# The last sums of an adaLN, fast-weight and expert block on one Trainium2 core: by halves of blocks, with the residual added on GpSimd

## The chip, the cores and the metric

The kernel runs on one core of a Trainium2 chip. The metric is the time of one launch on the device in microseconds. The engines are named as the profile names them: PE (TensorE), DVE (VectorE), ACT (ScalarE), POOL (GpSimd), SP (SyncE, which here only issues transfers). ACT and POOL issue transfers as well, each in a queue of its own, between their other instructions.

## The reference

The input x has 4 sequences of 1024 tokens of 128 features, 4096 tokens in all, in float32. Two sublayers follow each other, each with a layer norm whose shift and scale come from a small condition vector, and each with a gate (ga, gb) on what it adds to x:

```python
h = _layernorm(x) * (1 + ca) + sa
x = x + ga * _L0_attn_ref(h, ...)   # a two-layer network trained token by token, then asked
h = _layernorm(x) * (1 + cb) + sb
x = x + gb * _L0_ffn_ref(h, ...)    # 8 experts, the best 2 of each token, and a shared expert
```

The second sublayer is the one at issue. For each token the router's two largest probabilities are the gates of two experts; the sublayer's output is SCALE * (shared expert + gate0 * expert0 + gate1 * expert1).

## The kernel before, in words

The kernel has four stages: a front part with the first layer norm and the key and value projections; a scan that does the token-by-token training in windows (67 to 562 us of the profile, L498 to L700); the second layer norm and the router; and the experts. The order of every engine's instructions is the order of the program text.

**The scan** matters here only for what it shows of operations that run side by side. In each window DVE does, among others, `mT` from the two SBUF tensors `ae` and `th` (L621), `u` from a PSUM and an SBUF tensor (L530) and `ae` from a PSUM and an SBUF tensor (L650). POOL copies `dl` and `el` (L692, L693) and, in `add_changes`, does `ch` as a difference of two tensors (L547), `sq` and `va` as squares of one tensor (L548, L551) and three sums into `sums` (L555).

**The expert stage.** Tokens are sorted by expert into 71 tiles of 128 rows. For each tile, rows are gathered from `h_tab` (POOL, an indirect transfer, L1081), sent through the expert's two layers (L1108, L1112, L1120), and the result `yg` is scattered (POOL, L1125) into the DRAM table `y_tab`, at row 2 * token + k, k being 0 or 1 for the token's first or second expert. So a token's two rows lie beside each other, 1 KB together. The shared expert is added into `x_sb` in SBUF along the way (L945, L946), so that `x_sb` already holds all but the two experts' parts. The tensors `hs_all`, the shared expert's activations, are dead when the last tile is done.

**The last sums** are L1179 to L1203, and the change is there. The 4096 tokens are 8 blocks of 512, a block being 4 groups of 128 tokens over the partitions.

- Fetch (L1182): block j's rows of `y_tab` are fetched into the dead `hs_all[j]`, 512 KB in a transfer. Even blocks go by SP's queue, odd ones by ACT's. All eight are issued ahead of everything else. The first waits for the last scatter into `y_tab`.
- ACT multiplies the second expert's row by its gate in place (L1195), 128x128 in an operation, four for a block.
- DVE multiplies the first expert's row by its gate and adds (L1196, four for a block, into a tile `o`), multiplies the block by `gb` (L1199, 128x512), and adds `x_sb` (L1202, 128x512).
- Store (L1203): SP sends the 256 KB of `o` to the output. There are three buffers for `o`, so the fourth block waits until the first store has landed.

Every transfer tells its end on a semaphore; the program uses eight of them in turn for the transfers of SP and ACT, and a transfer that takes one up again waits until the earlier transfer on it has landed. After the eight fetches the eight stores take them up again.

Of the kernel before, what the change touches and what calls it, by code (L numbers as in the profile page):

```python
# [10 lines left out]
F32 = mybir.dt.float32  # L11
AF = mybir.ActivationFunctionType
ALU = mybir.AluOpType
# [4 lines left out]
P = 128  # L18
LR = 0.001
EPS = 1e-5  # L20
TOP_K = 2
# [4 lines left out]
def kernel(  # L26
# [23 lines left out]
    nc = tc.nc  # L50
    B, S, D = x.shape
# [5 lines left out]
    BLK = 4  # L57
    NBLK = NT // BLK
    BT = BLK * P
# [31 lines left out]
    x_sb = big.tile([P, NT, D], F32, name="x_sb")  # L91
# [4 lines left out]
    def tok(ap, j):  # L96
        b, i = j // half, j % half
        return ap[b, i * BT:(i + 1) * BT, :].rearrange("(c p) d -> p c d", p=P)
# [127 lines left out]
    gb_rep = const.tile([P, B, D], F32, name="gb_rep")  # L226
# [46 lines left out]
    with tc.tile_pool(name="scanbig", bufs=1) as sbig, tc.tile_pool(  # L273
        name="kdram", bufs=1, space=DRAM
# [19 lines left out]
        def span(i):  # L294

            return min(max(0, end(i) - WIN), S), min(end(i), S)
# [150 lines left out]
        for n in range(NBLK + 1):  # L447
            if n < NBLK:
                j = order[n]
# [43 lines left out]
        with tc.tile_pool(name="s_ps", bufs=1, space=PSUM) as sps, tc.manual_schedule():  # L493
# [71 lines left out]
            for i in range(NI):  # L565
                o, e = span(i)
# [133 lines left out]
                c = (i - GI) // GL + 1  # L700
# [11 lines left out]
        with tc.tile_pool(name="f_sb", bufs=1) as fp, tc.tile_pool(  # L712
            name="f_ps", bufs=1, space=PSUM
# [30 lines left out]
        with tc.If(again > 0):  # L744
            load_params(wa, wc, u, v, nc.scalar)
            half_bias(u)
            with tc.tile_pool(name="o_sb", bufs=1) as op_, tc.tile_pool(
                name="o_ps", bufs=1, space=PSUM
# [57 lines left out]
    y_tab = ffd.tile([TOP_K * NTOK, D], F32, name="y_tab")  # L806
    with ExitStack() as stage, tc.tile_pool(
        name="e_pa", bufs=3, space=PSUM
    ) as pa, tc.tile_pool(name="e_py", bufs=2, space=PSUM) as epy, tc.tile_pool(
        name="e_pt", bufs=2, space=PSUM  # L810
    ) as ept, tc.tile_pool(name="e_pl", bufs=1, space=PSUM) as epl, tc.manual_schedule():

        def small(name, shape, dtype=F32):
            return ffn.tile([P, *shape], dtype, name=name)
# [7 lines left out]
        gate = small("gate", [TOP_K, NT])  # L822
# [19 lines left out]
        ep = stage.enter_context(tc.tile_pool(name="q_sb", bufs=2))  # L842
# [44 lines left out]
        for s in range(NBLK + 5):  # L887
# [4 lines left out]
            if 0 <= s - 4 < NBLK:  # L892
                j = s - 4
# [9 lines left out]
        ep = stage.enter_context(tc.tile_pool(name="e_sb", bufs=2))  # L903
# [67 lines left out]
        at, d = 0, 1  # L971
        while d < NT:
# [3 lines left out]
            at, d = 1 - at, 2 * d  # L976
# [19 lines left out]
        at, d = 0, 1  # L996
        while d < NE:
# [4 lines left out]
            at, d = 1 - at, 2 * d  # L1002
# [42 lines left out]
        for n, (k, g) in enumerate(groups):  # L1045
            c = slice(g * GC, (g + 1) * GC)
# [103 lines left out]
        for h in range(2):  # L1150
            pg = bank(ept, "pg", "t", [NBLK // 2, P])
            for i in range(NBLK // 2):
                j = h * (NBLK // 2) + i
# [22 lines left out]
        down(*prev)  # L1176


        yts = []  # L1179
        for j in range(NBLK):  # L1180
            yt = hs_all[j][:, 0:2, :].rearrange("p f (c d) -> p (f c) d", d=TOP_K * D)
            (nc.scalar if j % 2 else nc.sync).dma_start(  # L1182
                yt,
                y_tab[j * BT * TOP_K:(j + 1) * BT * TOP_K, :].rearrange(
                    "(c p k) d -> p c (k d)", p=P, k=TOP_K
                ),
            )
            yts.append(yt)
        for j in range(NBLK):
            b, yt = j // half, yts[j]  # L1190
            o = ep.tile([P, BLK, D], F32, name="o", bufs=3)
            for i in range(BLK):
                c = j * BLK + i
                y0, y1 = yt[:, i, 0:D], yt[:, i, D:2 * D]
                nc.scalar.mul(y1, y1, gate[:, 1, c:c + 1])  # L1195
                nc.vector.scalar_tensor_tensor(  # L1196
                    o[:, i, :], y0, gate[:, 0, c:c + 1], y1, ALU.mult, ALU.add
                )
            nc.vector.tensor_tensor(  # L1199
                o, o, gb_rep[:, b:b + 1, :].to_broadcast([P, BLK, D]), ALU.mult  # L1200
            )
            nc.vector.tensor_tensor(o, o, x_sb[:, ts(j, BLK), :], ALU.add)  # L1202
            nc.sync.dma_start(tok(out, j), o)  # L1203


# [46 lines left out]
```

## Time and profile before

| what | us |
|---|---|
| median of three runs | 928.04 |
| lowest and highest of the three | 923.15, 930.83 |
| the profiled execution, its own time | 923.48 |
| its span, first to last instruction | 921.6 |
| last scatter of expert rows starts | 887.68 |
| first fetch of rows issued | 889.81 |
| first and last operation of the last sums on DVE | 895.53 to 917.91 |
| mean of L1196 (128x128), L1199 and L1202 (128x512) | 0.345, 0.691, 0.692 |
| mean of L1195 on ACT | 0.305 (2.44 for eight) |

Durations come from the profiled execution, whose time is 4.56 below the median of the runs. In a timeline a line is a run of equal operations: start, length from the first start to the last end, engine, line, operation, output <- inputs, shapes, how many (x4), and in brackets how long the engine sat idle before and what ended that. In a chain of waits each line is a start, a length and the step; the chain is followed back from the last instruction. "SPq" and "ACTq" are the queues that issue transfers, and "issue" is time in which nothing shown was waited for.

### The profile page before, as it was taken

Reading aid. Unit: us, or ns where it says so; the run is one execution under the profiler, and the core shown is the slowest. Engines: PE = TensorE matmul, PEld = TensorE weight load, DVE = VectorE, ACT = ScalarE, POOL = GpSimd, SP = SyncE. Lnnn points to the kernel's source line nnn. Section 1 sums busy time; section 2 is a strip of 40 time slices with the busy share of each in tenths; the row PEclk is TensorE's granted clock in tenths of the full one; section 3 lists DMA queues with packets and bytes.
Section 4 is the critical chain, followed back from the end, with each engine's and each line's share of the span. In section 5 each row is a group of like instructions: output and inputs, shape, how many; then the busy total and the mean of one; then the engine's idle time right before and its main releaser. Section 6 shows DMA issues by size and latency. Waiting matters only on the chain. (4 is left out here: it accounts for less than half of the span.)

```text
span 921.6 us, 21051 instructions
## 1 busy us (share of the span) xinstructions
PE 805.6 (87%) x6132; PEld 736.2 (80%) x6132; DVE 487.5 (53%) x1843; ACT 492.0 (53%) x1595; POOL 582.3 (63%) x1593
## 2 busy tenths in 40 slices
PE   4789999999999999999999997889888787887740
PEld 3456899999999999999999994546787787876740
DVE  5434566666666666666666663769422222212127
ACT  2554566666666666666666663674232333332332
POOL 7831578777877787778777883610266666666630
PEclk9999999999999999999999998999999999989775
DMA  4363201011111110111001000122166666656655
GB/s 126 85 210 109 82 24 25 22 43 25 25 24 40 25 25 22 41 25 25 23 23 25 23 4 1 35 59 92 29 195 208 198 211 197 216 182 204 196 174 167
DMA packets 77859, 79.84 MB, mean 87 GB/s; under 512 B 9904, under 2 KB 56990, under 8 KB 77744
## 3 DMA queue, kind: packets, MB, share of 16 engines
q1 hardware_dynamic: 68880, 65.58, 24.2%
q0 software_dynamic: 5600, 10.02, 3.8%
q10 hardware_dynamic: 3264, 2.89, 1.0%
q8 instruction: 50, 0.82, 0.4%
q14 instruction: 65, 0.53, 0.2%
HBM read 61.83 MB, written 17.53 MB: 86 GB/s over the span
## 5 line engine op out<-in xcount | busy, mean ns | idle before, releaser
L1112 ACT ACTIVATE hs<-ph,b1t 128x128 f32<-128x128 f32 x284 | 80.8, 370 | 148.1 <-PE pt L1099 69.1
L692 POOL COPY dl<-dz 24x128 f32<-24x128 f32 (+2 forms) x158 | 44.4, 281 | 123.8 <-DVE dz L669 123.8
L1081 POOL DMA_INDIRECT xg<-h_tab,toks_i x71 | 73.0, 1027 | 70.6 <-DVE toks_i L1077 49.1
L1125 POOL DMA_INDIRECT y_tab<-yg,rows_i x71 | 72.3, 1018 | 68.3 <-DVE xT L1101 52.7
L1120 PE MATMUL py<-w2t,hs 128*128 128x128 f32 x568 | 80.5, 286 | 31.1 <-issue 24.5
L530 DVE SCALAR_TENSOR_TENSOR u<-pu,u 128x130 f32<-128x130 f32 x158 | 46.5, 294 | 112.8 <-PE pu L517 112.8
L1120 PEld LDWEIGHTS py<-w2t,hs 128*128 128x128 f32 x568 | 72.0, 198 | 35.5 <-issue 28.3
L1124 DVE COPY yg<-py 128x128 f32<-128x128 f32 x71 | 20.6, 290 | 127.2 <-PE ps L940 68.3
L555 POOL TENSOR_TENSOR sums<-sums,sq 128x48 f32<-128x48 f32 (+2 forms) x315 | 86.4, 294 | 0.0
L1108 PE MATMUL ph<-xT,w1t 128*128 128x128 f32 x568 | 78.5, 283 | 5.3 <-DVE xT L1101 5.0
L633 ACT COPY ad<-z 128x128 f32<-128x128 f32 (+3 forms) x162 | 43.0, 265 | 66.4 <-PE z L631 66.4
L1108 PEld LDWEIGHTS ph<-xT,w1t 128*128 128x128 f32 x568 | 71.5, 197 | 7.6 <-DVE xT L1101 7.0
L596 PE MATMUL y<-nm,er 128*128 128x128 f32 (+3 forms) x322 | 73.4, 309 | 3.4 <-DVE nm L584 2.7
L498 PE MATMUL z<-kT,a 128*128 128x156 f32 (+3 forms) x324 | 72.9, 307 | 0.0
L539 ACT COPY c<-pv 128x128 f32<-128x128 f32 x158 | 42.0, 266 | 52.7 <-PE pv L535 49.8
L627 PE MATMUL y<-ae,c 128*128 128x128 f32 (+3 forms) x324 | 69.1, 295 | 0.0
L508 ACT ACTIVATE vb<-vT,v 128x128 f32<-128x128 f32 (+3 forms) x162 | 65.0, 401 | 1.2 <-DVE dr L656 0.9
L548 POOL TENSOR_TENSOR sq<-ch 128x104 f32<-128x104 f32 (+1 forms) x158 | 56.9, 360 | 12.4
L612 ACT ACTIVATE ae<-z,u 128x156 f32<-128x156 f32 (+3 forms) x162 | 62.8, 388 | 1.9 <-POOL el L693 0.9
L579 PE MATMUL z<-gm,dz 128*128 128x128 f32 (+3 forms) x322 | 62.9, 277 | 0.2
L662 PE MATMUL da<-v,ae 128*128 128x128 f32 (+3 forms) x324 | 62.9, 276 | 0.0
L551 POOL TENSOR_TENSOR va<-ae 128x48 f32<-128x48 f32 (+2 forms) x158 | 62.6, 396 | 0.0
(294 smaller groups left out, 2423.0 us busy)
## 6 DMA issues: line engine op xcount, KB each, us to landing
w1t<-in_e_w1t_dram SPq DMA_DIRECT2D x71, 256.0 KB
w2t<-in_e_w2t_dram SPq DMA_DIRECT2D x71, 256.0 KB
gm<-g_dram SPq DMA_DIRECT2D x151, 64.0 KB
g_dram<-gw SPq DMA_DIRECT2D x29, 206.0 KB
x_sb<-in_x_dram SPq DMA_DIRECT2D x8, 256.0 KB
k_dram<-kr SPq DMA_DIRECT2D x8, 256.0 KB
h_tab<-hr SPq DMA_DIRECT2D x8, 256.0 KB
hs_all<-y_tab ACTq DMA_DIRECT2D x4, 512.0 KB
```

The lines of the kernel that those rows point to most:

```text
L498: nc.tensor.matmul(z[:, 0:n], lhsT=wa, rhs=kc[:, o * B:o * B + n], start=True, stop=alone)
L508: nc.scalar.activation(vb[:, 0:n], vc[:, o * B:o * B + n], AF.Identity, bias=v[:, D:D + 1], scale=-1.0,)
L555: nc.gpsimd.tensor_tensor(t, t, x_[:, :, c0:c1], ALU.add)
L579: nc.tensor.matmul(z[:, 0:rn], lhsT=dz_p[0:ro, :], rhs=gms.pop(i)[0:ro, 0:rn], start=False, stop=True,)
L596: nc.tensor.matmul(y[:, 0:rn], lhsT=er_p[0:ro, :], rhs=nm[0:ro, 0:rn], start=True, stop=False,)
L627: nc.tensor.matmul(y[:, 0:rn], lhsT=wc, rhs=at[:, 0:rn], start=not prev, stop=True)
L662: nc.tensor.matmul(da[0:rn, :], lhsT=et[:, 0:rn], rhs=v[:, 0:D], start=not prev, stop=True)
L1081: nc.gpsimd.indirect_dma_start(out=xg_bufs[t % 6][:], out_offset=None, in_=h_tab[:, :], in_offset=bass.IndirectOffsetOnAxis(ap=toks_i[:, t ...
L1108: nc.tensor.matmul(ph[:, f, :], lhsT=w1t[:, ts(f, P)], rhs=xT, start=True, stop=True)
L1112: nc.scalar.activation(hs[:, f, :], ph[:, f, :], AF.Gelu_apprx_tanh, bias=b1t[:, t, f:f + 1])
L1120: nc.tensor.matmul(py, lhsT=hs[:, f, :], rhs=w2t[:, f, :], start=(f == 0), stop=(f == NFC - 1))
L1125: w = nc.gpsimd.indirect_dma_start(out=y_tab[:, :], out_offset=bass.IndirectOffsetOnAxis(ap=rows_i[:, t:t + 1], axis=0), in_=yg[:], in_off ...
```

## The change

The last sums go by halves of blocks, 256 tokens in place of 512.

- Each block's fetch becomes two of 256 KB, the first half by SP's queue and the second by ACT's: eight by each queue, sixteen in all, again issued ahead of everything else.
- `o` is a half, 128x256, in six buffers in place of three of 128x512.
- The multiplication by `gb` is done for a half (128x256, L1203 of the changed kernel), sixteen times in place of eight. The operations on 128x128 are as many as before (L1199 on ACT and L1200 on DVE there).
- `x_sb` is added by POOL (L1206 there, 128x256, sixteen times) in place of DVE.
- SP stores each half, 128 KB, as soon as POOL is done with it (L1209 there): sixteen stores.

```diff
+        HB = BLK // 2
...
-            (nc.scalar if j % 2 else nc.sync).dma_start(
-                yt,
-                y_tab[j * BT * TOP_K:(j + 1) * BT * TOP_K, :].rearrange(
-                    "(c p k) d -> p c (k d)", p=P, k=TOP_K
-                ),
-            )
+            for h, queue in enumerate((nc.sync, nc.scalar)):
+                r0 = (j * BLK + h * HB) * P * TOP_K
+                queue.dma_start(
+                    yt[:, ts(h, HB), :],
+                    y_tab[r0:r0 + HB * P * TOP_K, :].rearrange(
+                        "(c p k) d -> p c (k d)", p=P, k=TOP_K
+                    ),
+                )
...
-            o = ep.tile([P, BLK, D], F32, name="o", bufs=3)
-            for i in range(BLK):
-                c = j * BLK + i
-                y0, y1 = yt[:, i, 0:D], yt[:, i, D:2 * D]
...
-            nc.vector.tensor_tensor(
-                o, o, gb_rep[:, b:b + 1, :].to_broadcast([P, BLK, D]), ALU.mult
-            )
-            nc.vector.tensor_tensor(o, o, x_sb[:, ts(j, BLK), :], ALU.add)
-            nc.sync.dma_start(tok(out, j), o)
+            for h in range(2):
+                o = ep.tile([P, HB, D], F32, name="o", bufs=6)
+                for i in range(HB):
+                    c = j * BLK + h * HB + i
+                    y0, y1 = yt[:, h * HB + i, 0:D], yt[:, h * HB + i, D:2 * D]
...
+                nc.vector.tensor_tensor(
+                    o, o, gb_rep[:, b:b + 1, :].to_broadcast([P, HB, D]), ALU.mult
+                )
+                nc.gpsimd.tensor_tensor(
+                    o, o, x_sb[:, j * BLK + h * HB:j * BLK + (h + 1) * HB, :], ALU.add
+                )
+                nc.sync.dma_start(tok(out, j)[:, ts(h, HB), :], o)
```

More of the change, by code (lines that the diff above doesn't have):

```diff
@@ L1190 @@
             b, yt = j // half, yts[j]
-            o = ep.tile([P, BLK, D], F32, name="o", bufs=3)
-            for i in range(BLK):
-                c = j * BLK + i
-                y0, y1 = yt[:, i, 0:D], yt[:, i, D:2 * D]
-                nc.scalar.mul(y1, y1, gate[:, 1, c:c + 1])
-                nc.vector.scalar_tensor_tensor(
-                    o[:, i, :], y0, gate[:, 0, c:c + 1], y1, ALU.mult, ALU.add
-                )
-            nc.vector.tensor_tensor(
-                o, o, gb_rep[:, b:b + 1, :].to_broadcast([P, BLK, D]), ALU.mult
-            )
-            nc.vector.tensor_tensor(o, o, x_sb[:, ts(j, BLK), :], ALU.add)
-            nc.sync.dma_start(tok(out, j), o)
+            for h in range(2):
[3 more added lines that the diff above has]
+                    y0, y1 = yt[:, h * HB + i, 0:D], yt[:, h * HB + i, D:2 * D]
+                    nc.scalar.mul(y1, y1, gate[:, 1, c:c + 1])
+                    nc.vector.scalar_tensor_tensor(
+                        o[:, i, :], y0, gate[:, 0, c:c + 1], y1, ALU.mult, ALU.add
+                    )
+                nc.vector.tensor_tensor(
+                    o, o, gb_rep[:, b:b + 1, :].to_broadcast([P, HB, D]), ALU.mult
+                )
+                nc.gpsimd.tensor_tensor(
+                    o, o, x_sb[:, j * BLK + h * HB:j * BLK + (h + 1) * HB, :], ALU.add
+                )
+                nc.sync.dma_start(tok(out, j)[:, ts(h, HB), :], o)
 def kernel(**inputs):
```

## Prediction

> **What bounds the kernel now.** First the chain of waits, from the last gathered rows to the end. Its columns are start, duration and step, in us.
>
> ```profile
> 887.68 2.11 DMA y_tab<-yg,rows_i
> ...
> 889.85 5.23 DMA hs_all<-y_tab
> ...
> 898.24 7.00 DMA out_dram<-o
> ...
> 905.32 1.15 DVE o L1196 x4
> ...
> 917.22 0.69 DVE o L1202
> ```
>
> The expert stage ends at 887.68, and nothing ahead of 889.8 is touched by the change. What it can move is the last 32 us: the fetch of the expert rows from 889.85, VectorE from 895.53, one wait of VectorE for a store, and VectorE again until 917.91. The last store and the closing take 921.6 - 917.91 = 3.69. Next the timeline of that stretch.
>
> ```profile
> 895.10 2.44 ACT L1195 ACTIVATE hs_all<-hs_all,gate 128x128 f32<-128x128 f32 x8 [8.93 <-DMA hs_all<-y_tab]
> 895.53 1.23 DVE L1196 SCALAR_TENSOR_TENSOR o<-hs_all,gate 128x128 f32<-128x128 f32 x4 [8.49 <-ACT hs_all L1195]
> 898.13 1.13 DVE L1196 SCALAR_TENSOR_TENSOR o<-hs_all,gate 128x128 f32<-128x128 f32 x4
> 898.15 2.44 ACT L1195 ACTIVATE hs_all<-hs_all,gate 128x128 f32<-128x128 f32 x8 [0.61 <-DMA hs_all<-y_tab]
> ...
> 905.32 1.14 DVE L1196 SCALAR_TENSOR_TENSOR o<-hs_all,gate 128x128 f32<-128x128 f32 x4 [2.10 <-DMA out_dram<-o]
> ```
>
> Two things are to be seen. A block (four L1196, one L1199, one L1202) costs VectorE 2.51 us (905.32 to 907.83 and so on), so eight take 20.1; with the 2.1 of waiting that is the 22.4 from 895.53 to 917.91. And ScalarE is released in steps of 3.0 us (895.10, 898.15, then 901.16 and 904.12), one step for two blocks: the rows land at 1 MB per 3 us. The table of stretches says why:
>
> ```profile
> 892.00:894.00 2.00, 0.00 (x0) 0.00 (x0) 0.00 (x0) 0.00 (x0) 0.00 (x0) 0.50 1.04 358
> 902.00:904.00 2.00, 0.00 (x0) 0.00 (x0) 1.18 (x2) 1.61 (x6) 0.00 (x0) 0.50 1.10 350
> 906.00:908.00 2.00, 0.00 (x0) 0.00 (x0) 1.93 (x5) 0.57 (x2) 0.00 (x0) 0.50 0.02 6
> ```
>
> The last two columns are the DMA share and GB/s: the engines are full at about 350 GB/s while the 4.19 MB are fetched (12 us), and idle at 906. The first store, issued at 898.24, sits in SP's queue behind SP's fetches and lands only at 905.24. GpSimd does nothing here.
>
> **The change, part by part.**
>
> *Fetches: 16 of 256 KB for 8 of 512 KB.* The bytes and the rows are the same, and the DMA engines are full, so the rate stays: 1 MB per 3 us. What is new is a wait. In the built program of the changed kernel every transfer of SP and ACT signals on one of eight semaphores, and a transfer that reuses one waits for the transfer before it there. Eight fetches had one each. With sixteen, the fifth fetch of each queue (block 4) waits until the first one of that queue (block 0) has landed, and so on to the eighth, which waits for block 3. On SP only the last fetches and the stores are behind it (the eighth fetch at 898.1, the first store not before 900.9), and three 256 KB fetches per queue are still in flight, so the stream is not starved. On ACT all 32 multiplications stand behind it: the first can't start before block 3's second half is there. Blocks 0 to 3 are 2 MB, which had landed at 898.13 before (898.15 less the usual 0.03). Then the eighth fetch is issued (0.03 + 0.46, the shortest ACT issue of L1182, since this one has half the rows), one multiplication takes 0.41, and VectorE starts 0.03 after it: 898.13 + 0.03 + 0.46 + 0.03 + 0.41 + 0.03 = 899.1, against 895.53. That is 3.6 us lost at the head. After that ScalarE needs 0.61 per half and is always ahead.
>
> *The wait for an output buffer.* Six halves are the same space as three blocks. The first store again lands behind SP's fetches, 0.37 earlier for half the bytes at 350 GB/s: 904.87. VectorE reaches the seventh half at 904.9 or later (next part), so the 2.1 us of waiting are gone. They are no second gain: the late head has eaten them.
>
> *VectorE per half.* Two L1196 at a spacing of (1.13 - 0.344) / 3 = 0.262, so 0.262 + 0.344 = 0.61; 0.03 to the product (as from L1196 to L1199 now); the product of 128x256, which takes 0.424 (0.42 to 0.43 in every VectorE group of this size, L951 and L973 among them); the next half starts 0.08 before its end, as at 898.13. Together 0.98, or 15.7 for sixteen (15.8 to the end of the last). Eight blocks were 20.1: the removed L1202 gives 8 x 0.61 = 4.9 (897.52 to 898.13), and splitting L1199 takes 0.5 back.
>
> *The add on GpSimd.* It stands in GpSimd's queue behind the last scatter of rows, which was issued by 888.7, so nothing there holds it. The nearest rows are its differences at L547: 276 ns for 48 columns and 395 for 104, so 2.125 ns a column and 395 + 152 x 2.125 = 718 ns for 256. L548, which reads one tensor twice, gives 616. I take 0.72, since the add reads two tensors. It is below VectorE's 0.98, so GpSimd by itself does not become the bound. But does it run beside VectorE? The scan has the trial:
>
> ```profile
> 105.58 0.28 POOL L551 TENSOR_TENSOR va<-ae 128x56 f32<-128x56 f32 x1
> ...
> 106.32 0.31 POOL L555 TENSOR_TENSOR sums<-sums,va 128x56 f32<-128x56 f32 x1
> 106.39 0.38 DVE L621 SCALAR_TENSOR_TENSOR mT<-ae,th 128x128 f32<-128x128 f32 x1
> ```
>
> ```profile
> 403.85 0.29 DVE L621 SCALAR_TENSOR_TENSOR mT<-ae,th 128x128 f32<-128x128 f32 x1
> 403.86 0.41 POOL L551 TENSOR_TENSOR va<-ae 128x56 f32<-128x56 f32 x1
> 404.20 0.29 DVE L650 TENSOR_TENSOR ae<-y,vb 128x128 f32<-128x128 f32 x1
> 404.24 0.54 POOL L555 TENSOR_TENSOR sums<-sums,sq 128x56 f32<-128x56 f32 x2
> ```
>
> L621 reads two SBUF tensors. When it starts just ahead of L551, L551 takes 0.41 in place of 0.28; when L555 is 0.07 ahead, L621 takes 0.38 in place of 0.29. L650, which reads PSUM and SBUF, costs nobody anything. So the one that comes second is held. The Trainium skill ("SBUF — State Buffer", section "Who interferes with whom") has the rule, which speaks against this change: a VectorE instruction with two SBUF inputs and a GpSimd instruction that reads SBUF exclude each other, for the whole instruction. In the changed tail all three VectorE instructions of a half read two SBUF tensors (two halves of hs_all; o and gb_rep), so every add but the last falls between them. By the rule's words an add costs VectorE its whole 0.72: 15 x 0.72 = 10.8. By the row less: L621 was free at about 106.48, 0.16 after L555 began and 0.15 before its end, which fits the reading of its columns alone (56 x 2.125 = 0.12). I take the reading of 256 columns, 256 x 2.125 = 0.54; the low end is L548's slope, 256 x 1.68 = 0.43. So 15 x 0.54 = 8.1, and VectorE ends at 899.1 + 15.8 + 8.1 = 923.0. A half then takes 1.52, which also covers ScalarE (0.61) and SP's store issue (0.37).
>
> *The end.* The last add is on the path: 0.06 from VectorE to GpSimd (L669 to L692 in the scan) and 0.72. The last store has half the bytes, so 3.69 - 0.37 = 3.32. Sum: 923.0 + 0.06 + 0.72 + 3.32 = 927.1.
>
> *Sum.* 927.1 - 921.6 = 5.5 us slower: 3.6 at the head, 1.5 in VectorE's stretch (23.9 for 22.4: 4.4 less work, 2.1 less waiting, 8.1 of exclusion), 0.8 for the last add, 0.4 back at the store. On the profiled execution that makes 923.48 + 5.5 = 929.0; on the median of the three runs, 4.6 above it, 928.04 + 5.5 = 933.5.
>
> **Rivals.**
>
> *The add is free (0.10).* Then the halves take 0.98, the seventh half waits for the first store (899.1 + 5.9 = 905.0, as good as no wait), and the end is 899.1 + 15.8 + 0.78 + 3.32 = 919.0: 2.6 faster, 925.4. For it: GpSimd idles here. Against it: the two scan rows.
>
> *The exclusion costs more (0.18), the case on the slower side.* Place: the same 15 adds. If an add holds VectorE for its whole 0.72 and the hand-over costs what L551 shows at its end (403.86 + 0.41 is 0.13 after L621's), it is 0.85 each: 15 x 0.31 = 4.65 more, 10.1 slower, 938.2. It decides from 5.5 + 15 x 0.25 = 9.3 us, so from 0.79 per add. Against it: the 0.16 of L555.
>
> *The fetch wait does not hold ScalarE (0.10).* Block 0 alone is there 1.5 us earlier than blocks 0 and 1 were, at 893.6, and VectorE starts at 894.05. But at 1.52 a half it is at the seventh half by 903.2 and waits for the first store until 904.95; ten halves more, 9.8 + 0.08 + 9 x 0.54, then 0.78 + 3.32: 923.8, 2.2 slower, 930.2. So the early start is mostly lost again. Against it: the changed program's list of waits.
>
> **How the numbers follow.** The forecast has 0.62; its own range is 931.8 (lock 0.43) to 936.2 (0.72). About 1%, 9.3 us, is what a measurement of this kernel can tell from no change, as the three runs spread over 7.7. Of the cases only the dear exclusion passes it: slower 0.19; faster, by scatter alone, 0.02; within 0.79. The range goes from the free add, 925.4, to the dear exclusion, 938.5.
>
> **What would show it.** The first ScalarE multiplication near 898.7, behind four fetch waits; VectorE starting at 899.1 and halves at 1.5; L1200 and L1203 above 0.344 and 0.424, or gaps between them, wherever a GpSimd add runs; adds of 0.7 or longer; no wait for stores; the end near 927. Halves at 1.0 would mean the first rival, above 1.75 the second, a first multiplication near 893.6 the third. A stream clearly under 350 GB/s, or fetches starved by the new waits, would make the forecast wrong in a way that I have not priced.

## The result, and the profile after

The changed kernel takes 931.75 us (median of 20 runs, 928.85 to 940.82), the kernel before on the same chip 925.92 (20 runs, 923.15 to 932.92). The ratio is 1.0069, with a 95% interval of 1.0045 to 1.0093: 5.8 us slower by the medians.

The profiled execution was one of the longer ones, 938.76 us with a span of 937.1. Its first fetch is issued at 898.05 and not at 889.81, but nothing ahead of the fetch is changed, and in a second profile of the same kernel (below) the fetch is at 890.59. So I compare the stretch from the first fetch's issue to the end of the span, T below. It was 921.6 - 889.81 = 31.8 before and is 937.1 - 898.05 = 39.05 after, 7.3 longer. The second profile gives 39.61. The medians differ by less, 5.8, with an interval of 4.2 to 8.6. T comes from one profile of each kernel; the two profiles of the changed kernel differ by 0.6, so a difference of that size between two T says little. In all the kernels below, the change of T and the change of the time (by the ratio) agree within 1.5 us.

The timeline of that stretch:

```profile
898.05 8.64 ACTq L1185 DMA_DIRECT2D hs_all<-y_tab  x8
898.09 8.24 SPq L1185 DMA_DIRECT2D hs_all<-y_tab  x8
906.74 9.45 ACT L1199 ACTIVATE hs_all<-hs_all,gate 128x128 f32<-128x128 f32 x32 [11.96 <-DMA hs_all<-y_tab]
907.18 0.64 DVE L1200 SCALAR_TENSOR_TENSOR o<-hs_all,gate 128x128 f32<-128x128 f32 x2 [11.52 <-DMA hs_all<-y_tab]
907.85 0.42 DVE L1203 TENSOR_TENSOR o<-o,gb_rep 128x256 f32<-128x256 f32 x1
908.20 1.08 DVE L1200 SCALAR_TENSOR_TENSOR o<-hs_all,gate 128x128 f32<-128x128 f32 x2
908.37 0.76 POOL L1206 TENSOR_TENSOR o<-o,x_sb 128x256 f32<-128x256 f32 x1 [11.46 <-DVE o L1203]
909.15 22.38 SPq L1209 DMA_DIRECT2D out_dram<-o  x16
909.31 0.42 DVE L1203 TENSOR_TENSOR o<-o,gb_rep 128x256 f32<-128x256 f32 x1
...
929.85 0.42 DVE L1203 TENSOR_TENSOR o<-o,gb_rep 128x256 f32<-128x256 f32 x1
930.41 0.72 POOL L1206 TENSOR_TENSOR o<-o,x_sb 128x256 f32<-128x256 f32 x1 [0.74 <-POOL o L1206]
```

Three things are to be seen. ACT issues fetches until 906.69, and its first multiplication comes only then: 8.7 after the first fetch, against 5.3. The first pair of L1200 takes 0.64, when GpSimd has nothing yet to do; each later pair takes 1.08, and an add of GpSimd lies over it. And the last operation of VectorE ends at 930.27, the last add at 931.13, the span at 937.1: 6.0 us after the last add, where before 3.7 us lay behind VectorE's last operation.

It is not the issuing itself that keeps ACT so long. Its first four fetches are issued by 900.08, the other four follow one by one at 901.66, 903.16, 905.20 and 906.33. The row of the issues (count; shortest, median and longest in ns; first and last start) makes some 3.3 us for all eight, out of 8.6:

```profile
L1185 ACTq DMA_DIRECT2D hs_all<-y_tab x8: 366/416/484, 898.1 to 906.3; - x8
```

In SP's queue, where the profile names the waits, four fetches waited for earlier fetches, 4.6 us in all (total, times, longest):

```profile
SPq L1185 <- DMA hs_all<-y_tab: 4.6, 4, 1.3
```

The chain of waits, from VectorE's first operation on:

```profile
901.37 5.83 DMA hs_all<-y_tab
907.19 0.64 DVE o L1200 x2
...
908.20 1.09 DVE o L1200 x2
...
928.73 0.94 DVE o L1200 x2
929.67 0.71 issue
930.38 0.75 POOLq L1254
```

Its first line is a fetch that landed at 907.20, and the profile puts VectorE's first wait down to it. But the half that VectorE does first had landed when SP's fifth fetch, which waits for it, went out at 901.37; what came at 907.15 was ScalarE's first product (906.74 and 0.41 for one multiplication), and the second profile puts the same wait down to ScalarE. No store is on the chain: the wait for a buffer is gone. In the table of stretches the stream of rows is as full as before (the last two columns):

```profile
904.00:906.00 2.00, 0.00 (x0) 0.00 (x0) 0.00 (x0) 0.00 (x0) 0.00 (x0) 0.50 1.09 353
912.00:914.00 2.00, 0.00 (x0) 0.00 (x0) 1.93 (x5) 2.00 (x8) 0.80 (x2) 0.50 0.39 115
931.00:937.00 6.00, 0.00 (x0) 0.00 (x0) 0.00 (x0) 0.00 (x0) 0.13 (x1) 0.50 0.09 25
```

The last row is the 6 us in which no engine computes. What ends them is in the closing instructions (line 1254 is the launch; the columns are count, shortest, median and longest in ns, first and last start):

```profile
L1254 POOLq DRAIN  x3: 46/115/5833, 930.4 to 936.8; - x3
L1254 SPq DRAIN  x3: 7/7/7, 933.1 to 936.5; - x3
```

SP has its last store back at 933.1 and waits. GpSimd's drain is counted from the start of its last add, 930.4, and lasts 5.83 us, to 936.2, which is 5.1 beyond the end of the add; the engines then meet and the program ends. Before, the same drain took 6.65 us from 887.1, with the last scatter (887.68 to 888.66) inside it, and was over by 893.8, before VectorE began its first sum at 895.53:

```profile
L1248 POOLq DRAIN  x3: 46/115/6645, 887.1 to 921.3; - x3
```

### The profile page after: what moved, and what is told of

Read it like the earlier page. It is cut to its first block, busy times and chain, and to the rows that moved or that the text cites. A ratio compares the mean times of both kernels' runs of the same rounds, so it can differ in the third digit from the quotient of the medians.

```text
span 937.1 us, 21115 instructions
## 1 busy us (share of the span) xinstructions
PE 812.0 (87%) x6132; PEld 741.7 (79%) x6132; DVE 489.5 (52%) x1843; ACT 490.8 (52%) x1595; POOL 593.5 (63%) x1609
```

## The experiments

My theory had three parts by now: fetches that wait hold ScalarE (head), GpSimd's add and VectorE exclude each other (lock), and GpSimd's drain lies bare behind its last add (closing). The rivals: smaller transfers are slow, VectorE waits for buffers, the long closing was chance. The runs lie on several chips. On two of them the kernel before takes 885 us, on the one of "mended without GpSimd" and of the second profile of the changed kernel 924; each time is compared with the kernel before on the same chip. T is compared across chips: the kernel before with one small copy, on a chip of 885 us, has the same head and the same stretch of VectorE as the kernel before had on one of 926.

| kernel | ratio to before (95%) | T | first multiplication of ACT | VectorE, start to end | end after the last add, sum or copy |
|---|---|---|---|---|---|
| before | 1 | 31.8 | 5.3 | 22.4 | 3.7 |
| changed | 1.0069 (1.0045 to 1.0093) | 39.05 | 8.7 | 23.1 | 6.0 |
| changed, second profile | 1.0100 (1.0019 to 1.0181) | 39.6 | 9.3 | 23.1 | 6.0 |
| add on VectorE | 1.0035 (1.0009 to 1.0062) | 35.6 | 9.2 | 23.2 | 2.8 |
| whole-block fetches | 1.0039 (1.0011 to 1.0067) | 36.2 | 5.2 | 23.8 | 5.9 |
| operands in PSUM | 1.0003 (0.9982 to 1.0025) | 32.3 | 9.0 | 15.6 | 6.0 |
| last four adds on VectorE | 1.0044 (1.0017 to 1.0070) | 35.9 | 9.2 | 23.5 | 2.8 |
| all fetches by SP | 1.0061 (1.0037 to 1.0085) | 37.4 | 2.8 | 27.4 | 6.0 |
| before and one small copy | 1.0031 (1.0006 to 1.0055) | 34.2 | 5.3 | 22.4 | 5.9 |
| all mended | 0.9916 (0.9888 to 0.9945) | 24.4 | 2.8 | 17.9 | 2.9 |
| before, no wait for stores | 0.9979 (0.9950 to 1.0008) | 29.8 | 5.4 | 20.2 | 3.7 |
| mended without GpSimd | 0.9985 (0.9956 to 1.0013) | 29.3 | 2.8 | 23.2 | 2.9 |

**The add back on VectorE.**

```diff
-                nc.gpsimd.tensor_tensor(
+                nc.vector.tensor_tensor(
                     o, o, x_sb[:, j * BLK + h * HB:j * BLK + (h + 1) * HB, :], ALU.add
```

> Halves, two fetch queues and sixteen stores kept, only the add goes back to VectorE. T is the stretch from the first fetch's issue to the end of the span: 31.8 in the kernel before, 39.05 in the changed one. Theory (late head by the fetch waits, exclusion of VectorE and GpSimd, GpSimd's closing after its last add): the head stays, so VectorE starts 9.1 after the first fetch; a half takes 0.98 + 0.375 = 1.355, sixteen 21.7, no add of GpSimd at the end and no long closing: T = 9.1 + 21.7 + 3.3 = 34.1, 2.3 slower than the kernel before. Rival (GpSimd is innocent, the halves and their stores cost the time): T stays near 39.

T is 35.6, 1.5 over the forecast: VectorE started 9.6 after the first fetch, not 9.1, and a half took 1.44, not 1.355 (I had left out that each operation of a half waits for the one before); the end was 0.5 shorter. The timeline of one half:

```profile
869.02 0.61 DVE L1200 SCALAR_TENSOR_TENSOR o<-hs_all,gate 128x128 f32<-128x128 f32 x2
869.66 0.42 DVE L1203 TENSOR_TENSOR o<-o,gb_rep 128x256 f32<-128x256 f32 x1
870.12 0.43 DVE L1206 TENSOR_TENSOR o<-o,x_sb 128x256 f32<-128x256 f32 x1
870.46 0.61 DVE L1200 SCALAR_TENSOR_TENSOR o<-hs_all,gate 128x128 f32<-128x128 f32 x2
```

869.02 to 870.46 is 1.44, where the changed kernel needs 1.455: an add on GpSimd costs VectorE what the add on VectorE would. So the move saved nothing in the stretch, and the 3.5 us between the two kernels are the last add (0.86) and the longer closing (3.2), less the 0.5 by which this head was later. GpSimd is not innocent, but the whole of the 5.8 is not its doing: this kernel still has the late head.

**Whole-block fetches.** The fetch lines of the kernel before (even blocks by SP, odd ones by ACT), the rest as changed.

```diff
-            for h, queue in enumerate((nc.sync, nc.scalar)):
-                r0 = (j * BLK + h * HB) * P * TOP_K
-                queue.dma_start(
+            (nc.scalar if j % 2 else nc.sync).dma_start(
...
```

> Fetches of whole blocks, even ones by SP and odd ones by ACT, as in the kernel before; the rest as changed. Theory: no fetch waits, VectorE starts 5.7 after the first fetch as before; halves at 1.455 as in the changed kernel; the seventh half waits for the first store until 15.1; then ten halves, the last add and the long closing: T = 15.1 + 14.6 + 6.8 = 36.5. So of the 3.4 us at the head 2.5 come back, the rest goes to the wait for a buffer. Rival (the late start is not the fetch waits but smaller transfers): the start is then also early, and the two are not told apart by this run alone, but by the one with all fetches on SP. Rival (the fetches have no part): T = 39.

T is 36.2 for 36.5. The head is back at 5.2, VectorE waits 1.2 us for the first store, and the rest is as in the changed kernel: 3.5 us come back at the head, VectorE's stretch is 0.7 longer, T is 2.8 shorter.

**Operands in PSUM.** ScalarE writes its products into a PSUM tile, gb is copied into PSUM once, and the two multiplications of a half come ahead of VectorE's operations.

```diff
+        gbp = bank(epl, "gbp", "l", [B, D])
+        nc.vector.tensor_copy(gbp, gb_rep)
...
+                yp = bank(pa, "yp", "a", [HB, D])
...
-                    nc.scalar.mul(y1, y1, gate[:, 1, c:c + 1])
+                    nc.scalar.mul(yp[:, i, :], yt[:, h * HB + i, D:2 * D], gate[:, 1, c:c + 1])
...
-                        o[:, i, :], y0, gate[:, 0, c:c + 1], y1, ALU.mult, ALU.add
+                        o[:, i, :], y0, gate[:, 0, c:c + 1], yp[:, i, :], ALU.mult, ALU.add
...
-                    o, o, gb_rep[:, b:b + 1, :].to_broadcast([P, HB, D]), ALU.mult
+                    o, o, gbp[:, b:b + 1, :].to_broadcast([P, HB, D]), ALU.mult
```

> As changed, but ScalarE writes the second expert's product into PSUM and gb lies in PSUM, so each VectorE operation of the last sums has only one SBUF tensor; GpSimd's adds are as they were. Theory of exclusion (two SBUF inputs against GpSimd's reads): VectorE's halves fall from 1.455 to 0.98, sixteen take 15.8, T = 9.1 + 15.8 + 6.8 = 31.7, 7.3 less than the changed kernel. Rival (VectorE is held by buffers, by semaphores or by GpSimd's work as such): halves stay at 1.45, T = 39.

The timeline, with the adds of GpSimd as long as before:

```profile
869.39 0.60 DVE L1205 SCALAR_TENSOR_TENSOR o<-hs_all,gate,yp 128x128 f32<-128x128 f32 x2
869.55 0.73 POOL L1211 TENSOR_TENSOR o<-o,x_sb 128x256 f32<-128x256 f32 x1 [0.25 <-DVE o L1208]
870.02 0.42 DVE L1208 TENSOR_TENSOR o<-o,gbp 128x256 f32<-128x256 f32 x1
870.36 0.60 DVE L1205 SCALAR_TENSOR_TENSOR o<-hs_all,gate,yp 128x128 f32<-128x128 f32 x2
```

The add lies over the pair as in the changed kernel, and the pair takes 0.60 in place of 1.08. A half is 0.97, T 32.3 for 31.7. This settles the lock: the adds, the buffers of the sums and the stores are the same, each VectorE operation reads one SBUF tensor less, and 7.5 us of VectorE's stretch are gone. (T falls by 6.7, as VectorE starts 0.7 later, behind two multiplications in place of one.) The longest L1200 and L1205 say it in one row each, for the changed kernel and for this one:

```profile
L1200 DVE SCALAR_TENSOR_TENSOR o<-hs_all,gate x32: 343/352/824, 907.2 to 929.0; 128x128 f32<-128x128 f32 x32
```

```profile
L1205 DVE SCALAR_TENSOR_TENSOR o<-hs_all,gate,yp x32: 339/340/346, 863.6 to 878.4; 128x128 f32<-128x128 f32 x32
```

The second of a pair is held: 0.824 - 0.343 = 0.48, fifteen times. One such second of the changed kernel, and the add beside it (the pair starts at 911.10):

```profile
911.37 0.82 DVE L1200 SCALAR_TENSOR_TENSOR o<-hs_all,gate 128x128 f32<-128x128 f32 x1
911.27 0.77 POOL L1206 TENSOR_TENSOR o<-o,x_sb 128x256 f32<-128x256 f32 x1 [0.69 <-DVE o L1203]
```

**The last four halves added by VectorE.**

```diff
-                nc.gpsimd.tensor_tensor(
+                (nc.vector if j >= NBLK - 2 else nc.gpsimd).tensor_tensor(
```

> As changed, but the last four halves are added by VectorE. Theory (GpSimd closes only about 5.1 us after its last instruction): GpSimd's last add now ends some 5 us ahead of VectorE's end, its closing is hidden; VectorE: 9.1 + 12 x 1.455 + 4 x 1.355 = 32.0, end 3.3 later, T = 35.3. Rival (the long closing of the changed kernel's profile belongs to that execution): then this run's end after the last VectorE operation is 3.3 too, but so is that of other runs that end with GpSimd's add; the run with all fetches whole shows that.

T is 35.9 for 35.3. The end lies 2.8 behind VectorE's last operation. GpSimd's last add ends 8.2 us before the end, and its drain is covered.

**One small copy at the end of the kernel before.**

```diff
+        gz = ep.tile([P, 1], F32, name="gz", bufs=1)
+        nc.gpsimd.tensor_copy(gz, o[:, BLK - 1, D - 1:D])
```

> The kernel before with one more instruction at the very end: GpSimd copies one column of the last block's sum, after VectorE's last operation. Nothing reads it. Theory (GpSimd closes about 5.9 us after its last instruction, whatever that is): VectorE ends at 28.1 as before, GpSimd at 28.4, the end at T = 34.3, 2.5 slower than before. Rival (the long closing comes from the many adds or from the transfers behind them): T = 31.8, no change.

T is 34.2, 2.4 longer than before, for a copy of 128 numbers that nothing waits for. Its row in the timeline, and the drain behind it:

```profile
878.30 0.18 POOL L1205 COPY gz<-o 128x1 f32<-128x1 f32 x1 [29.27 <-DVE o L1202]
```

```profile
L1250 POOLq DRAIN  x3: 46/115/5293, 878.3 to 884.1; - x3
```

The copy ends at 878.48 and the drain at 883.6: 5.1 us. In the changed kernel it is 936.2 - 931.13 = 5.1 as well, and in the kernel before, behind its last scatter, 893.8 - 888.66 = 5.1. So it depends neither on the adds nor on their number. What GpSimd does in these 5.1 us, no run shows.

**All fetches by SP.**

```diff
-            for h, queue in enumerate((nc.sync, nc.scalar)):
+            for h, queue in enumerate((nc.sync, nc.sync)):
```

> As changed, but SP's queue fetches both halves of every block, so that no fetch stands ahead of ScalarE's multiplications. T is the stretch from the first fetch's issue to the end of the span, 31.8 in the kernel before and 39.05 in the changed one. Theory (the late head is ScalarE held by fetches that wait for a semaphore): the first multiplication falls from 8.7 after the first fetch to 4 or less, earlier than the 5.3 of the kernel before; but at 1.455 a half VectorE is at the seventh half by 13 and waits for the first store until about 15.1; then ten halves, the last add and GpSimd's closing: T = 15.1 + 14.6 + 0.85 + 6.0 = 36.5. Rival (transfers of half the size are slower and make the head late): the first multiplication stays at 8 or later, T = 39.

The first multiplication comes 2.75 after the first fetch, with transfers of the same size: the late head was ScalarE behind its own fetches, not the size. But T is 37.4, 0.9 over the forecast, and the time is not clearly better than that of the changed kernel, because VectorE then waits for a buffer:

```profile
861.96 0.72 POOL L1206 TENSOR_TENSOR o<-o,x_sb 128x256 f32<-128x256 f32 x1 [0.69 <-DVE o L1203]
866.32 0.61 DVE L1200 SCALAR_TENSOR_TENSOR o<-hs_all,gate 128x128 f32<-128x128 f32 x2 [4.44 <-ACT hs_all L1199]
```

The wait is booked to ScalarE, whose product had long been there; the seventh half needs the first store's buffer. That store stands behind all sixteen fetches in SP's queue and is issued at 860.55; VectorE goes on 16.2 after the first fetch, where I had put 15.1. In the two mended kernels below, with the same fetches but no buffer to wait for, there is no such wait.

**All mended.** All fetches by SP, operands in PSUM, the last four adds on VectorE, and the sums written into the dead half of `hs_all`, so that no buffer is waited for:

```diff
-                o = ep.tile([P, HB, D], F32, name="o", bufs=6)
+                o = hs_all[j][:, 2 + h, 0:HB * D].rearrange("p (c d) -> p c d", d=D)
```

> All three costs taken away at once: SP fetches all halves, the operands of VectorE lie in PSUM as in the run before, the sums go into the dead half of hs_all so that no store is waited for, and VectorE adds the last four halves so that GpSimd's closing is hidden. Theory: VectorE starts at about 4.3, takes 12 x 0.97 + 4 x 1.43 = 17.4, ends at 21.7, and the end comes 2.8 later: T = 24.5, 7.3 faster than the kernel before (0.8%). Rival (the stretch is bounded by the 6.3 MB of fetches and stores at 350 GB/s, 18 us from 1.7 on, plus a landing): T not under 22, which this is above; if the stores after the fetches run at half that rate, T = 28.

T is 24.4 for 24.5, the median 877.3 for 884.9: faster than the kernel before by 0.8%, and so than the changed one. Two more runs say what in it counts. The kernel before with its sums in `hs_all`:

```diff
-            o = ep.tile([P, BLK, D], F32, name="o", bufs=3)
+            o = hs_all[j][:, 2, :].rearrange("p (c d) -> p c d", d=D)
```

> The kernel before with the sums written into the dead half of hs_all, so that no block waits for a store; nothing else. Theory (the 2.1 us wait for a buffer is on the path and is all that more buffers are worth): T = 31.8 - 2.1 = 29.7. Rival (the first store's landing is needed for something else, or the stores then collide with the fetches): T = 31.8 or near.

T is 29.8, as forecast; in the time the interval still holds 1. And the mended kernel without GpSimd and PSUM (the first run's add, SP's fetches, the sums in `hs_all`):

> The run with everything mended, but without GpSimd: SP fetches all halves, the sums lie in the dead half of hs_all, VectorE does all adds and its operands are in SBUF as in the changed kernel. Theory (GpSimd's add is worth its 0.46 a half only where it does not exclude VectorE): VectorE starts at 3.2, a half takes 1.44 as in the run with VectorE's adds, sixteen 23.0 + 0.1, the end 2.8 later: T = 29.1, 2.7 faster than the kernel before and 4.6 slower than with PSUM operands and GpSimd. Rival (the gain of the mended run came from the early start and the missing waits alone): T = 24.5 to 26.

T is 29.3 for 29.1, and the rival is out: the early start and the missing waits are worth 2.5 us here, which the time cannot tell from nothing, and GpSimd beside an unhindered VectorE is worth the other 4.9. PSUM operands by themselves are worth nothing: in the last halves of the mended run, where VectorE adds as well, a half takes 1.43 with them, and 1.44 here without.

**The changed kernel again**, on the chip of the last run, unaltered:

> The changed kernel once more, unaltered, beside the others: its profiled execution was a long one (938.76 for a median of 931.75). Theory (what is longer there lies ahead of the first fetch, the stretch of the last sums is the same in every execution): T = 39.1 to 39.6, GpSimd's last add to the end 5.97. Rival (the long closing belongs to that execution): T about 36.4.

T is 39.6, and 5.95 us lie behind the last add. Its time, from few runs, is 1.010 of the kernel before (1.002 to 1.018). The long closing is no matter of one execution.

## Why the prediction was right, and where it was off

The forecast was 5.5 us slower, 933.5 on the median of the three runs then known; measured are 5.8 and 931.75. Its sums come out, except that the dear exclusion stands once as 938.2 and once as 938.5; 928.04 + 5.5 + 4.65 is 938.2. The mechanism stood step by step, with one term badly sized and two slightly, in opposite directions.

- **Head**: forecast 3.6 us lost (VectorE's start 9.3 after the first fetch for 5.7). Measured 9.13 and 9.70 in the two profiles: 3.4 and 4.0. The run with SP's fetches confirms why.
- **The wait for a buffer**: forecast gone without being a gain. It is gone, and the runs with the early head show it come back: 1.2 us with whole-block fetches, 4.4 with SP's.
- **VectorE's halves**: forecast 0.98 by themselves. Measured 0.97, with operands in PSUM.
- **Exclusion**: forecast 0.54 for each add, between the 0.43 of one row's slope and the 0.72 of the rule's words ("SBUF — State Buffer" in the Trainium skill, section "Who interferes with whom", has the loser blocked for the whole instruction). Measured 1.455 - 0.97 = 0.485, with the add at 0.72. So the rule names the right pair of instructions, but the price here is two thirds of the add. Two things make the difference. In the pair shown above the add starts at 911.27, while the first operation still runs, and its first 0.1 us cost nothing: the second is due only at 911.37. And the second ends at 912.19; with the 0.343 that it takes when free, it got going near 911.85, 0.2 ahead of the end of the add (912.04), much as in the scan (0.15). So the add blocks VectorE for the first 0.58 of its 0.77. That this time goes by the columns that GpSimd reads fits both places (0.58 for 256 columns, 0.16 for 56 in the scan), but one size of add was run here, so it isn't shown. VectorE's stretch was 23.1 for a forecast 23.9.
- **The end**: this is the term that failed. "The last store has half the bytes, so 3.69 - 0.37 = 3.32" behind the last add; measured 5.97. I asked what the store would cost and not what GpSimd needs behind its last instruction. The page of the kernel before could have told me: the closing instructions there have a drain of GpSimd of 6.6 us, harmless only because it began at 887.1. The store's own part was too dear in the other direction: with half the bytes the end lies 2.8 behind VectorE's last operation, 0.9 less, not 0.37.

The measured parts of T add up: 3.4 (head) + 0.7 (VectorE's stretch) + 0.86 (last add) + 2.3 (5.97 for 3.69) = 7.3. The forecast of 5.5 for the same stretch missed 2.7 at the end and had 0.8 too much in the exclusion and 0.2 at the head. So its nearness to the 5.8 of the medians is in part luck: errors that offset each other, and 1.5 us between the medians and T. That the medians show 5.8 and not 7.3 is within their interval; whether 1.5 us come back elsewhere, the runs don't say.

Of the rivals, the free add is out (it exists, but only with PSUM operands), the dear exclusion is out (0.485 for its 0.85), and ScalarE is held by the fetch waits.

## What to carry to other kernels

Before work is moved to GpSimd, count the SBUF tensors that VectorE's operations around it read: beside operations with two of them the move gave nothing (1.455 us a half for 1.44), and with one of the two in PSUM it gave the whole add (0.97). Let GpSimd not be the last engine to work, for its closing then lies bare. And when transfers are split, look which of them now wait for an earlier one, and which engine's work stands behind them in the queue.

## What the runs showed of the hardware

GpSimd's drain at the end of the program took 5.1 us from the end of its last instruction, be that a scatter, an add of 256 columns or a copy of one; where it ended last (an add or the copy), the program ended 0.9 us later. With all sixteen fetches of 256 KB in SP's queue, the first released ScalarE 2.75 us after its issue, against 5.3 with eight of 512 KB in two queues. And of the three VectorE operations of a half, GpSimd's add held the second (0.82 for 0.34, fifteen times) and neither the first nor the third, which kept their 0.34 and 0.42.
